# Layer 0's softmax in a four-layer graph kernel: one exponential over the whole tile, with the maximum subtracted and the rows summed by VectorE

## The chip, the cores and the metric

The kernel runs on one core of a Trainium2 chip. The metric is the device time of one execution in microseconds (us), as the median of several executions. A profile comes from one execution of its own, recorded by the hardware profiler. In it PE is TensorE (PEld its weight loads), DVE is VectorE, ACT is ScalarE, POOL is GpSimd and SP is SyncE; "L278" is line 278 of the kernel before the change.

## The reference, cut to what matters

Four graph layers stand one behind the other, each with a residual and a layer norm. `x` has 128 graphs of 64 nodes with 256 features, all float32. The change touches the first layer, a graph attention:

```python
def _L0_gnn_ref(h, adj_matrix, W, a):
    Wh = jnp.einsum('bnf,fo->bno', h, W)
    a1, a2 = (a[:Fout, 0], a[Fout:, 0])
    s1 = Wh @ a1
    s2 = Wh @ a2
    e = s1[:, :, None] + s2[:, None, :]
    e = jnp.where(e >= 0, e, ALPHA * e)
    e = jnp.where(adj_matrix[None] == 0, -jnp.inf, e)
    attention = jax.nn.softmax(e, axis=-1)
    return jnp.einsum('bij,bjo->bio', attention, Wh)
...
x = _layernorm(x + _L0_gnn_ref(x, adj, L0_gnn_W, L0_gnn_a), axis=-1)
x = _layernorm(x + _L1_gnn_ref(x, ...), axis=-1)
```

The second layer is an attention over a list of 512 edges with four heads; the third (two matrix products with batch normalisation) and the fourth (two graph products and LSTMs over windows) come later in time.

## The kernel before

The tokens are cut into 16 blocks of 512 (8 graphs). A block is four tiles of 128 tokens, each with two graphs, so that a softmax tile `e` of layer 0 is 128 partitions by 4 x 128 elements: in each of the four 128 x 128 pieces a row is one node and the columns are the nodes of two graphs, those outside the node's own graph and edges masked with -1e30.

Layer 0 of a block is cut into steps. `l0_a` (L238) brings the transposed input, `l0_b` (L247) makes `Wh` with the two scores, `l0_c` (L260) builds `e`: transposes on TensorE (L264), mask and sums on VectorE (L267), leaky ReLU (L269) and the negated row maximum `mx` (L271). `l0_x` (L274) is the exponential: ScalarE runs it four times, once for each 128 x 128 piece (L278), because its bias operand holds one number for each partition and each piece has its own maximum; each of the four also adds up its rows into `sm`. VectorE then takes the reciprocal `ri` (L281). `l0_d` (L283) transposes `e` on TensorE (L287) and copies it to SBUF (L289), and `l0_e` (L291) multiplies by `Wh` (L297), scales by `ri`, adds the residual (L300) and does the layer norm (`layernorm`, L88, with its last step on GpSimd, L100).

Layer 1 of a block: `l1_t` transposes the block (L227, L228); `l1_qv` makes, for half a block at a time, the queries (product L324, copies by ScalarE L334, subtractions by VectorE L335, small copies into `spad` L336) and the values (product L327, copy by ScalarE L337). `l1_graph` multiplies a graph's queries by the edge matrix (L361) into one of two PSUM buffers `z`, which ScalarE empties with a ReLU into `u` (L363); `reduce_heads` adds up the heads (L352). `l1_softmax`, `l1_sums` and `l1_weights` (L368 to L414) are the softmax over edges, once for two blocks. `v_m`, `v_a`, `v_b`, `v_c` (L416 to L474) apply the weights to the values of a block some rounds back: `v_a` is the product L432 and its copies `yT` (L436), `v_b` the product L446, the residual and a layer norm, `v_c` the product L467 for layer 2 and its copy (L471). All PSUM tiles but `z` and the edges' sums come from three banks named `m`, which are given out in turn, so that a product can wait for an earlier tile's last copy.

The order is written out by hand. The loop at L701 makes one round for each block q, with eight graph steps, and between two of them the steps listed in `between` (L703): in one round layer 1's graphs of block q, layer 1's queries and values of block q+1, and layer 0 of block q+2 stand side by side. `step` (L679) ties each step behind the last TensorE instruction of the step before it. Otherwise the instructions of an engine are put in order by a scheduler at build time, by readiness and the order of the code; at run time each engine works off its own list in order. Where `l0_x` stands depends on the round:

```python
def behind(do, q):
    if q < NQ:
        with tc.issue_after([t for t in nc.cur_bb.bb.instructions
                             if t.engine == mybir.EngineType.Activation][-1]):
            do(q)
```

S is q // 2 - 1 in even rounds and -1 in odd ones. In rounds with S >= 0 (even q from 2 on) `l0_x` is put behind the latest ScalarE instruction that was written, which is the values' copy of the first half block (L337). In the others (odd q, and q = 0) it is a step of its own ahead of the queries. The softmaxes of blocks 0 and 1 run ahead of the loop.

Of the kernel before, what the change touches and what calls it, by code (L numbers as in the profile page):

```python
# [8 lines left out]
F32 = mybir.dt.float32  # L9
F32R = mybir.dt.float32r  # L10
I32 = mybir.dt.int32
AF = mybir.ActivationFunctionType
OP = mybir.AluOpType
AX = mybir.AxisListType
# [3 lines left out]
P = 128  # L18
# [9 lines left out]
PQ = 4  # L28
# [13 lines left out]
def kernel(ctx: ExitStack, tc: tile.TileContext, i, out):  # L42
    nc = tc.nc

    const = ctx.enter_context(tc.tile_pool(name="const", bufs=1))
    small = ctx.enter_context(tc.tile_pool(name="small", bufs=4))
# [83 lines left out]
    with ExitStack() as two:  # L130
# [13 lines left out]
        def bank(shape, name="m", bufs=3):  # L144
            return (psm if name == "m" else ps).tile([P] + shape, F32, name=name, bufs=bufs)
# [71 lines left out]
        def own(q, shape, name):  # L217

            return work.tile(shape, F32, name=name, bufs=1) if q else su.tile(shape, F32, name)
# [16 lines left out]
        L0 = {}  # L236
# [37 lines left out]
        def l0_x(q):  # L274
            e, mx = L0[q]["e"], L0[q]["mx"]
            sm = small.tile([P, PQ], F32, name="sm")
            for c in range(PQ):
                nc.scalar.activation(e[:, c, :], e[:, c, :], AF.Exp, bias=mx[:, c:c + 1],  # L278
                                     accum_out=sm[:, c:c + 1])
            ri = L0[q]["ri"] = small.tile([P, PQ], F32, name="ri")  # L280
            nc.vector.reciprocal(ri, sm)  # L281

        def l0_d(q):  # L283
            e = L0[q]["e"]
            p_ = bank([PQ, P])
            for c in range(PQ):
                nc.tensor.transpose(p_[:, c, :], e[:, c, :], ident)  # L287
            eT = L0[q]["eT"] = own(q, [P, PQ, P], "eT")
            nc.scalar.activation(eT, p_, AF.Copy)  # L289
# [76 lines left out]
        ld, sm = {}, {}  # L366
# [202 lines left out]
        setup_order()  # L569
        l0_c(0)  # L570
        l0_x(0)
        l0_a(1)
        setup_ends()
        l0_b(1)
        l0_d(0)
        setup_gather()
        setup_queries()
        l0_e(0)
        l0_c(1)
        l0_x(1)  # L580
        setup_signs()
        l0_d(1)
        l1_t(0)
        l1_qv(0, 0)
# [94 lines left out]
        def step(do, n, *more):  # L679
            if not 0 <= n < NQ:  # L680
                return
            traced = nc.cur_bb.bb.instructions
            first = len(traced)
            if queue:
                with tc.issue_after(queue[-1]):
                    do(n, *more)
            else:
                do(n, *more)
            mine = [t for t in traced[first:] if t.engine == mybir.EngineType.PE]
            queue.extend(mine[-1:])  # L690
# [6 lines that stand above are left out]
# [4 lines left out]
        for q in range(NQ):  # L701
            S = q // BPS - 1 if q % BPS == 0 else -1
            between = [  # L703
                [(l0_e, q + 1), (l0_a, q + 2)],
                [(sums, q if q else -1), (l1_softmax, S)],
                [(l1_sums, S), (l0_b, q + 2)],
                [(v_b, q - LAG - 1)],
                [(l1_t, q + 1), (l1_weights, S), (l0_c, q + 2)] + [(l0_x, q + 2)] * (S < 0),
                [(sums, q), (l1_qv, q + 1, 0)] + [(lambda n: behind(l0_x, n), q + 2)] * (S >= 0),
                [(v_c, q - LAG - 1), (v_a, q - LAG)],  # L710
                [(l0_d, q + 2), (l1_qv, q + 1, 1)],
            ]
            for b in range(GQ):
                step(l1_graph, q, b)
                for do, n, *more in between[b]:
                    step(do, n, *more)
                if setup:
                    setup.pop(0)()
        sums(q)
        S = NQ // BPS - 1  # L720
# [256 lines left out]
        q = NQ - LAST - 1  # L977
# [16 lines left out]
        bias = wd.tile([P, SKIP, 8], F32, name="bias")  # L994
# [1010 lines left out]
```

## Time and profile before

| | before |
|---|---|
| median of 3 runs | 2036.22 us (2034.6 to 2041.47) |
| the profiled execution | 2039.12 us |
| its span from first to last instruction | 2037.3 us |
| granted TensorE clock, mean | 0.985 |
| TensorE busy | 1940.1 us (95%) |
| VectorE, ScalarE, GpSimd busy | 1248.0, 988.0, 880.0 us |
| four exponentials of all blocks, L278 | 64 of 390 ns (median), and 64 accumulator reads of 187 ns |
| row maximum, L271 | 16 of 685 ns |
| reciprocal, L281 | 16 of about 175 ns, VectorE idle 20.2 us before them |

The loop of layers 0 and 1 lies between about 66 and 560 us of the span, and a round takes about 30 us. A line of the timeline gives the start and the length in us, the engine, the line of the kernel, the operation, the tiles written and read, their shapes and how many; in square brackets stands how long the engine was idle before it and whose result ended that. A row of the groups ends with the busy time in all, the mean of one in ns, and the idle time before such instructions with the releasers.

### The profile page before, as it was taken

The page shows a single profiled execution, that of the slowest core. Times are in us where ns is not written, and L with a number is a line of the kernel's source. Part 1 is how long each engine was busy: PE and PEld are TensorE (multiplying, and loading weights), DVE is VectorE, ACT ScalarE, POOL GpSimd, SP SyncE. Part 2 cuts the span into 40 slices and gives each one's busy share as a digit, 9 for nine tenths or more (in the row PEclk, how much of TensorE's full clock was granted, in tenths as well). Part 3 has the DMA queues.
Part 4 walks back from the last instruction along what each step waited for, and adds up shares of the span by engine and source line. Part 5 has one row for each costly group of instructions (what it writes and reads, how often), then busy time and mean ns, then how long its engine had stood idle before and what let it go on. Part 6 is the DMA issues. An engine that isn't in the chain of part 4 may idle for free.

```text
span 2037.3 us, 31496 instructions
## 1 busy us (share of the span) xinstructions
PE 1940.1 (95%) x11447; PEld 1337.8 (66%) x11447; DVE 1248.0 (61%) x2763; ACT 988.0 (48%) x1892; POOL 880.0 (43%) x1017
## 2 busy tenths in 40 slices
PE   5999999999999999899999999999999999999996
PEld 4667777766554445477678577667577668578685
DVE  7456565565456555765557865557775557664566
ACT  2766666666345633644343644333544333543333
POOL 1123333333445544564645543435543445444264
PEclk8999999999999998999999999999999999999999
DMA  5344443332302025433243243133143032132022
GB/s 129 85 67 65 83 68 55 66 45 39 51 22 60 38 93 185 148 139 107 86 162 92 66 155 136 39 132 88 58 152 121 24 111 66 47 119 78 0 62 73
DMA packets 236539, 173.84 MB, mean 85 GB/s; under 512 B 150624, under 2 KB 213600, under 8 KB 233056
## 3 DMA queue, kind: packets, MB, share of 16 engines
q1 hardware_dynamic: 234528, 169.86, 29.5%
q8 instruction: 90, 1.47, 0.3%
q0 software_dynamic: 1024, 1.05, 0.2%
q10 hardware_dynamic: 832, 0.92, 0.1%
q14 instruction: 65, 0.53, 0.1%
HBM read 110.18 MB, written 61.60 MB: 84 GB/s over the span
## 4 chain that ended last, share of the span: by engine, by line
PE 73%; DVE 14%; ACT 5%; DMA 3%; issue 3%; POOL 2%; SPq 1%; DVEq 0%; POOLq 0%; ACTq 0%
PE l L1728 27%; PE l L1684 8%; PE pz L845 4%; PE l L1463 4%; PE m L253 3%; PE pz L774 3%; PE m L324 3%; PE e L352 2%; PE m L446 2%; PE g L1362 2%; PE m L327 2%; PE z L361 2%; PE g L1350 2%; PE pz L1043 2%; DVE cell L1642 1%
## 5 line engine op out<-in xcount | busy, mean ns | idle before, releaser
L1728 PE MATMUL l<-hs,wh 128*128 128x256 f32 (+1 forms) x896 | 276.0, 399 | 3.7 <-DVE hs L1592 3.1
L1728 PE MATMUL l<-xs,wx 128*128 128x256 f32 (+1 forms) x896 | 276.2, 399 | 2.9 <-DVE gate L1747 2.7
L1743 ACT ACTIVATE kept<-l 128x256 f32<-128x256 f32 (+1 forms) x224 | 88.8, 403 | 333.2 <-PE l L1728 331.8
L86 POOL TENSOR_TENSOR ln_rs<-ln_rs,mhalf 128x2 f32<-128x2 f32 (+2 forms) x98 | 85.5, 873 | 367.4 <-DVE ln_rs L98 366.9
L1728 PE MATMUL l<-H,wx 128*128 128x256 f32 (+1 forms) x672 | 210.5, 402 | 4.3 <-DVE gate L1756 3.4
L1728 PE MATMUL l<-hid,wh 128*128 128x256 f32 (+1 forms) x672 | 208.7, 399 | 0.0
L1728 PEld LDWEIGHTS l<-hs,wh 128*128 128x128 f32 x896 | 169.1, 190 | 47.1 <-DVE hs L1592 5.7
L1728 PEld LDWEIGHTS l<-xs,wx 128*128 128x128 f32 x896 | 168.9, 190 | 46.1 <-issue 2.8
L1761 ACT ACTIVATE gate<-gate,bias 128x512 f32<-128x512 f32 (+1 forms) x280 | 170.6, 657 | 40.7 <-DVE gate L1752 34.8
L1684 PE MATMUL l<-H,wx 128*128 128x256 f32 (+5 forms) x672 | 185.2, 431 | 4.9 <-DVE H L116 2.7
L363 ACT ACTIVATE u<-z 128x1024 f32<-128x1024 f32 x128 | 130.3, 1026 | 68.8 <-PE z L361 67.7
L1684 PEld LDWEIGHTS l<-H,wx 128*128 128x128 f32 x672 | 118.8, 190 | 65.5 <-issue 34.2
L1728 PEld LDWEIGHTS l<-H,wx 128*128 128x128 f32 x672 | 125.7, 190 | 42.6 <-DVE gate L1756 7.4
L1728 PEld LDWEIGHTS l<-hid,wh 128*128 128x128 f32 x672 | 127.2, 190 | 32.0 <-issue 2.9
L1751 POOL TENSOR_TENSOR gate<-gate,kept 128x256 f32<-128x256 f32 (+1 forms) x84 | 65.1, 775 | 144.9 <-DVE kept L1749 136.2
L335 DVE TENSOR_TENSOR qs<-m,qs 64x256 fp32r<-64x256 f32 x128 | 54.0, 422 | 106.3 <-ACT qs L334 104.4
L361 PE MATMUL z<-gath_r,qs 128*128 128x512 f32 x256 | 100.4, 480 | 9.3 <-ACT u L363 8.9
L1756 DVE TENSOR_TENSOR gate<-l,gate 128x256 f32<-128x256 f32 (+1 forms) x112 | 50.0, 446 | 88.4 <-POOL gate L1751 64.3
L1596 POOL TENSOR_TENSOR hs<-hid 128x256 f32<-128x256 f32 (+1 forms) x28 | 26.0, 929 | 170.1 <-DVE hid L1628 87.0
L1650 ACT ACTIVATE gate<-cell 128x512 f32<-128x512 f32 (+1 forms) x88 | 58.6, 666 | 83.6 <-DVE cell L1642 61.5
L1638 POOL TENSOR_TENSOR cell<-gate,cell 128x512 f32<-128x512 f32 (+1 forms) x56 | 75.4, 1367 | 28.4 <-ACT gate L1761 28.4
L1745 DVE TENSOR_TENSOR gate<-l,kept 128x256 f32<-128x256 f32 (+1 forms) x112 | 49.1, 438 | 59.7 <-ACT gate L1761 32.6
(380 smaller groups left out, 4097.6 us busy)
## 6 DMA issues: line engine op xcount, KB each, us to landing
wx<-sums SPq DMA_DIRECT2D x9, 2048.0 KB
wh<-sums SPq DMA_DIRECT2D x9, 1792.0 KB
way<-st SPq DMA_DIRECT2D x54, 256.0 KB
st<-way SPq DMA_DIRECT2D x216, 64.0 KB
xin<-in_x SPq DMA_DIRECT2D x16, 512.0 KB
ld<-table SPq DMA_DIRECT2D x16, 512.0 KB
x_dram<-y SPq DMA_DIRECT2D x16, 512.0 KB
x2r<-x_dram SPq DMA_DIRECT2D x32, 256.0 KB
```

Of the source, the lines that this page charges most:

```text
L86: nc.gpsimd.tensor_tensor(dst, dst, mhalf[:, :n], OP.pow)
L253: nc.tensor.matmul(p_, xT[:, k, c * P:(c + 1) * P], w0[:, k, :], start=k == 0, stop=k == KD - 1)
L361: nc.tensor.matmul(z[:, k, :], L1[q]["qs"][c][:, s, k * P:(k + 1) * P], gath_r, start=True, stop=True)
L363: nc.scalar.activation(u, z, AF.Relu)
L845: nc.tensor.matmul(self.bank[at], lhs, rhs, start=first and n == 0, stop=n == len(self.terms) - 1, skip_group_check=True)
L1463: nc.tensor.matmul(self.bank[at], lhs, rhs, start=new, stop=True, skip_group_check=True)
L1638: nc.gpsimd.tensor_tensor(c, t, c, OP.mult)
L1684: nc.tensor.matmul(b, w.raw[0][:, k, at, m, :], x, start=k == 0, stop=k == KD - 1)
L1728: nc.tensor.matmul(self.banks[j], lhs, rhs, start=src == 0, stop=src == 1)
L1743: nc.scalar.activation(self.keep(j), b, AF.Copy)
L1751: e.tensor_tensor(t[0][:, 1], t[0][:, 1], k[5], OP.add)
L1761: given(lambda: nc.scalar.activation(dst, dst, f, bias=b))
```

## The change

In the loop (q from 2 on) VectorE adds the negated maximum to the whole tile `e`, the maximum being repeated along each row of 128; ScalarE does one exponential over 128 x 512 without bias and without row sums; and VectorE sums the rows, in `l0_d`, ordered behind the VectorE instruction that was written last, and takes the reciprocal there. Blocks 0 and 1, ahead of the loop, keep the old form. In all rounds `l0_x` is now put behind the values' copy, so in odd rounds and round 0 too.

```diff
         def l0_x(q):
             e, mx = L0[q]["e"], L0[q]["mx"]
             sm = small.tile([P, PQ], F32, name="sm")
-            for c in range(PQ):
-                nc.scalar.activation(e[:, c, :], e[:, c, :], AF.Exp, bias=mx[:, c:c + 1],
-                                     accum_out=sm[:, c:c + 1])
+            if q < 2:
+                for c in range(PQ):
+                    nc.scalar.activation(e[:, c, :], e[:, c, :], AF.Exp, bias=mx[:, c:c + 1],
+                                         accum_out=sm[:, c:c + 1])
+            else:
+                nc.vector.tensor_add(e, e, mx[:, :, None].to_broadcast([P, PQ, P]))
+                nc.scalar.activation(e, e, AF.Exp)
+            L0[q]["sm"] = sm
+
+        def l0_d(q):
+            e, sm = L0[q]["e"], L0[q]["sm"]
             ri = L0[q]["ri"] = small.tile([P, PQ], F32, name="ri")
-            nc.vector.reciprocal(ri, sm)
-
-        def l0_d(q):
-            e = L0[q]["e"]
+            if q < 2:
+                nc.vector.reciprocal(ri, sm)
+            else:
+                with tc.issue_after([t for t in nc.cur_bb.bb.instructions if t.engine == mybir.EngineType.DVE][-1]):
+                    nc.vector.reduce_sum(sm, e, axis=AX.X)
+                nc.vector.reciprocal(ri, sm)
             p_ = bank([PQ, P])
...
-                [(l1_t, q + 1), (l1_weights, S), (l0_c, q + 2)] + [(l0_x, q + 2)] * (S < 0),
-                [(sums, q), (l1_qv, q + 1, 0)] + [(lambda n: behind(l0_x, n), q + 2)] * (S >= 0),
+                [(l1_t, q + 1), (l1_weights, S), (l0_c, q + 2)],
+                [(sums, q), (l1_qv, q + 1, 0)] + [(lambda n: behind(l0_x, n), q + 2)],
```

## The prediction

> **What bounds the kernel now.** I read the page's busy slices first, then the busy times by stretch, TensorE's timeline with its idle times, ScalarE's timeline in one block of each kind, and last the price rows. Round q (a pass of the loop at L701) carries the softmax of block q+2, so it is 14 rounds, 0 to 13, that change, all between 66 and 470 us.
>
> ```profile
> PE   5999999999999999899999999999999999999996
> ACT  2766666666345633644343644333544333543333
> ```
>
> ```profile
> 274.00:305.00 31.00, 30.08 (x278) 22.05 (x274) 21.80 (x50) 20.54 (x46) 12.03 (x15) 1.00 0.25 51
> 305.00:336.00 31.00, 29.00 (x272) 21.66 (x269) 16.18 (x48) 20.36 (x45) 11.83 (x15) 1.00 0.45 73
> ```
>
> The first numbers after the length are TensorE, its weight loads, VectorE, ScalarE, GpSimd. TensorE is the bound: it idles 0.9 us in an odd round (274 to 305) and 2.0 us in an even one (305 to 336). ScalarE is busy two thirds of the time. So freed ScalarE time is worth only what it takes from those idle times. TensorE's timeline shows where they are:
>
> ```profile
> 78.74 0.65 PE L287 MATMUL m<-ident,e 128*128 128x128 f32 x4 [0.34 <-ACT v L337]
> 220.12 1.15 PE L324 MATMUL m<-wq,tT 128*128 128x260 f32 x4 [0.56 <-ACT yT L436]
> 250.96 0.75 PE L361 MATMUL z<-gath_r,qs 128*128 128x512 f32 x2 [1.79 <-ACT u L363]
> 252.37 2.10 PE L324 MATMUL m<-wq,tT 128*128 128x260 f32 x4 [0.22 <-ACT yT L436]
> ```
>
> Even rounds 4 to 12 lose 2.0 us here (1.79+0.22 in round 6), odd rounds 5 to 13 lose 0.56 (L324 at 220.12 in round 5; L361 follows u at 218.39 almost without a wait), all waiting for ScalarE. An even round (6) and an odd one (5) on ScalarE:
>
> ```profile
> 247.51 0.38 ACT L334 ACTIVATE qs<-m 64x256 fp32r<-64x256 f32 x1
> 247.91 0.40 ACT L278 ACTIVATE e<-e,mx 128x128 f32<-128x128 f32 x1
> 249.89 1.02 ACT L363 ACTIVATE u<-z 128x1024 f32<-128x1024 f32 x1
> 250.81 1.02 ACT L471 ACTIVATE A<-z 128x1024 f32<-128x1024 f32 x1
> 251.71 1.09 ACT L436 ACTIVATE yT<-m 128x512 f32<-128x512 f32 x2
> ```
>
> ```profile
> 213.55 0.39 ACT L278 ACTIVATE e<-e,mx 128x128 f32<-128x128 f32 x1
> 216.91 0.38 ACT L334 ACTIVATE qs<-m 64x256 fp32r<-64x256 f32 x1
> 217.32 1.02 ACT L363 ACTIVATE u<-z 128x1024 f32<-128x1024 f32 x1
> ```
>
> In the even round the four exponentials stand directly ahead of the u that TensorE waits for. In the odd round they run 3.4 us earlier, while ScalarE would otherwise wait for queries. This difference decides the forecast.
>
> **What the Trainium skill says.** "ScalarE: Activation LUTs", section "What ACT_TABLE_LOAD costs": an ACTIVATE takes about 280 ns + 0.833 ns per element with a pointer bias, 186 ns + 0.833 without, overlaps by 93 ns, and a table load takes 1283 ns. The trace agrees: 392 ns at 128 with bias (387 by the page), 630 at 512 without (613), load 1283. "SBUF — State Buffer", section "Who interferes with whom": a VectorE instruction with two SBUF inputs contends with GpSimd reads, a tensor_reduce doesn't. The trace fits: the two-input add L380 takes 868 ns beside GpSimd's L100, the same size with one input in PSUM (L373) 691. The price rows (after the bar: busy us, mean ns of one, idle before it):
>
> ```profile
> L278 ACT ACTIVATE e<-e,mx 128x128 f32<-128x128 f32 x56 | 21.8, 392 | 0.6 <-DVE mx L271 0.4
> L381 ACT ACTIVATE e<-e 128x512 f32<-128x512 f32 x7 | 4.4, 630 | 12.2 <-DVE e L380 12.2
> L271 DVE TENSOR_REDUCE mx<-e 128x4 f32<-128x512 f32 x14 | 9.6, 686 | 0.5
> L269 DVE SCALAR_TENSOR_TENSOR e<-e 128x512 f32<-128x512 f32 x14 | 9.8, 697 | 0.5
> L380 DVE TENSOR_TENSOR e<-e,dn 128x512 f32<-128x512 f32 x7 | 6.1, 868 | 0.2
> ```
>
> **The change, part by part.** *Prices.* Removed per block: four exponentials, started 0.39 apart and ended by a 0.19 accumulator read, 1.65 us of ScalarE. Added: one of 0.63. ScalarE is relieved of 1.0 us a block, 14 us in all. VectorE gains an add and a row sum. The sum is a reduction like L271, 0.69. The add's broadcast operand is not in this trace; it cannot be cheaper than L269's 0.69 and I bound it above by 0.95 (the slowest two-input row of this size, L116 on wh, 953 ns); I take 0.69 in even rounds, where GpSimd isn't in L100 at that moment, and 0.87 in odd ones, where L100 runs from 212.16 to 214.33. VectorE: +1.4 to 1.6 us a block, 21 us in all.
>
> *Order.* From the order of instructions on each engine of both kernels: TensorE and GpSimd are unchanged; on SyncE a few input loads swap places, all two blocks ahead of their use, taken as nothing (if a load came late, its cover of some 20 us would have to go). VectorE runs maximum, add, the remaining query subtractions, sum, reciprocal. On ScalarE the exponential now stands after the values' copy (L337) and the last query copy (L334) in every round, and u follows.
>
> *Even rounds 4 to 12.* In round 6 the maximum ends at 246.85, a subtraction at 247.30, so the add at about 248.03, only 0.1 after the old start of the exponentials. One exponential lets u start 0.54 later (0.63 less 0.09 overlap), 248.6 instead of 249.89. TensorE's wait of 1.79 falls to about 0.5. Next late is the chain u, small copy L336 (now behind u), A, yT: A moves from 250.81 to 249.85, so L324 starts at 251.4 instead of 252.37. Gain 0.95 a round, not 1.3; five rounds, **-4.75**. Were the add 0.95, the gain would be 0.7.
>
> *Round 2* has waits of 0.84 and 0.37 of the transposes L287 for the exponentials; with the exponential from 132.6 to 133.25 they end near 133.9 instead of 134.8: **-0.8**.
>
> *Odd rounds 5 to 13.* With the exponentials gone from the front, the queries' chain still ends where TensorE lets it: the second half's product starts at 213.93, its copy follows 1.08 later as in even rounds (215.01), then subtraction, L336 and the last copy at 216.05, values' copy 216.45, exponential 217.06, L336, u at 217.84. It was 217.32: u is 0.5 later, and L361 waits that long. A follows without the L336 that stood between, so it and yT are 0.2 later, and TensorE's L324 with them: **+1.0** in five rounds. Round 3, retimed in the same way, +0.3.
>
> *Rounds 0 and 1* have neither A nor yT, and the transposes L287 come early: 78.74 and 103.73, released by the values' copy. Now they wait for the exponential behind it: in round 1 it would run from 103.7 to 104.3, +0.65. In round 0 the exponential brings the table load of 1.28 us (needed after the logarithm at L645), which ran early and now stands after the last query copy (78.67): 79.95, then the exponential to 80.6: +1.9. Together **+2.55**.
>
> *The new wait.* The sum waits on VectorE for the exponential; behind it are the reciprocal and the second half's subtractions, which come 4 us later (VectorE idled 4.84 before the one at 254.92). The reciprocal's reader, L300, comes 9 us later. Cost nothing; without that idle time, up to 0.9 a block. The old wait of the reciprocal (20.2 us of VectorE idle in all) hid nothing either.
>
> **Sum.** -4.75-0.8+1.0+0.3+2.55 = -1.7 us. The profiled execution took 2039.12 (span 2037.3), 2.9 above the median of 2036.22; 2037.4 there, 2034.5 for the median. The later stages only move with it.
>
> **The rivals.** *ScalarE's whole saving arrives.* If what TensorE waits for is ScalarE's sum of work in every round, 14 rounds give 1.0 each: 2036.2-14 = 2022. For it: every wait above names ScalarE, and waits of up to 15.6 us are there (5 x 2.0 + 5 x 0.56 + 2.8 in rounds 0 to 3). Against it: odd rounds' exponentials fill idle ScalarE time. Half of it would be 2029.
>
> *Slower: the odd rounds' add is held up by GpSimd.* The first subtraction of the queries now stands behind the add on VectorE. By the chain above it may end as late as 213.95 before anything moves, so the add, from 213.0, decides at 0.94 us. If it waits until L100's four instructions are over (214.33), u starts at 218.9, 1.6 late, and L324 1.25 late instead of 0.2: +6.25 for five rounds, in sum +3.5, 2039.7. For it: L380 and L100 slow each other (L100 takes 801 ns in one place, 558 in another). Against: they interleave, L380 lost only 0.18.
>
> *It doesn't do what it says*, the waits being tied to something else: 2036.2. Against it: the order shows the exponential moved in all 14 rounds.
>
> **How the numbers follow.** Forecast 0.62 (2034.5, itself 2031 to 2038 by the add's bounds, 1.3 us, by halving or doubling the losses of rounds 0 and 1, and by the spread of the runs, 2034.6 to 2041.5). ScalarE's whole saving or half of it 0.22; slower 0.12; nothing 0.04. 0.3% is 6 us, about what a measurement of this kernel tells from no change: 2030.1 and 2042.3. Faster by more: 0.20 of the second case and a little of the first, 0.22; slower by more: half of the slower case, 0.07; the rest 0.71. The range reaches into both: 2028.5 to 2040.5.
>
> **What would show it.** Right: TensorE's idle before L361 in even rounds near 0.5 and before L324 near 0.5; in odd rounds 0.6 before L361 and 0.25 before L324; L287 waiting about 2 us for e in round 0, 0.6 in round 1; the add at 0.7 to 0.9. Wrong: odd rounds without any wait (first rival), or the add over 0.94 with late subtractions (second).

## The result and the profile after

Over 20 executions of each the changed kernel took 2032.99 us (median; 2030.11 to 2038.06) and the kernel before 2040.53 us (2034.03 to 2044.41). The ratio on record is 0.9971, with a 95% interval from 0.9962 to 0.998: about 6 us faster (the medians themselves are 7.5 us apart), where 1.7 was forecast. The profiled execution took 2033.86 us (span 2032.1) at a clock of 0.986; before it was 2039.12 (2037.3) at 0.985. Lines of the kernel after stand 10 lower in the file from `l0_d` on: L287 is now L297, L361 is L371, L324 is L334, L363 is L373, L436 is L446, L467 is L477; the exponential is L283, the add L282, the row sum L293.

The page's busy slices of TensorE and ScalarE, after:

```profile
PE   5899999998999989899999999999999999999996
ACT  2666666666345633634343644333544333543333
```

They hardly differ from those of before. What changed is too small for a slice of 51 us; the page's sums of busy time show the work that was exchanged: ScalarE 988.0 to 973.8 us (-14.2; 14 were forecast), VectorE 1248.0 to 1268.4 (+20.4; 21 were forecast). Busy time by stretches of 31 us, after (TensorE, its weight loads, VectorE, ScalarE, GpSimd), about an odd and an even round:

```profile
270.00:301.00 31.00, 29.86 (x274) 22.22 (x274) 23.19 (x51) 19.62 (x39) 12.40 (x14) 1.00 0.25 50
301.00:332.00 31.00, 29.86 (x278) 22.07 (x271) 18.36 (x53) 19.52 (x39) 12.66 (x17) 1.00 0.44 73
```

TensorE now idles 1.1 us in both kinds of round, where it was 0.9 and 2.0. Its timeline after, at the places that the prediction showed (rounds 0, 1, 5 and 6):

```profile
77.81 0.66 PE L297 MATMUL m<-ident,e 128*128 128x128 f32 x4 [2.14 <-ACT e L283]
103.11 0.66 PE L297 MATMUL m<-ident,e 128*128 128x128 f32 x4 [0.85 <-ACT e L283]
216.96 0.75 PE L371 MATMUL z<-gath_r,qs 128*128 128x512 f32 x2 [0.54 <-ACT u L373]
218.36 1.14 PE L334 MATMUL m<-wq,tT 128*128 128x260 f32 x4 [0.22 <-ACT yT L446]
248.02 0.75 PE L371 MATMUL z<-gath_r,qs 128*128 128x512 f32 x2 [0.61 <-ACT u L373]
249.75 1.14 PE L334 MATMUL m<-wq,tT 128*128 128x260 f32 x4 [0.54 <-ACT yT L446]
```

The 1.79 us ahead of u's reader in round 6 is 0.61, and the 0.22 ahead of L334 has grown to 0.54: the second in the chain is now what is late. In round 5 the wait for u, hardly there before, is 0.54. In round 0 the transposes wait 2.14 us. ScalarE and VectorE in round 6 and in round 5, after:

```profile
245.56 0.69 DVE L282 TENSOR_TENSOR e<-e,mx 128x512 f32<-128x512 f32 x1
246.29 0.63 ACT L283 ACTIVATE e<-e 128x512 f32<-128x512 f32 x1 [0.17 <-DVE e L282]
246.94 1.02 ACT L373 ACTIVATE u<-z 128x1024 f32<-128x1024 f32 x1
248.19 1.02 ACT L481 ACTIVATE A<-z 128x1024 f32<-128x1024 f32 x1
249.11 1.08 ACT L446 ACTIVATE yT<-m 128x512 f32<-128x512 f32 x2
```

```profile
210.25 2.59 POOL L100 TENSOR_SCALAR y<-y,ln_rs 128x256 f32<-128x256 f32 x4
211.11 0.78 DVE L282 TENSOR_TENSOR e<-e,mx 128x512 f32<-128x512 f32 x1
215.04 0.62 ACT L283 ACTIVATE e<-e 128x512 f32<-128x512 f32 x1
215.88 1.02 ACT L373 ACTIVATE u<-z 128x1024 f32<-128x1024 f32 x1
```

In round 5 the add ran beside GpSimd's L100 and took 0.78 us, and its own reader did not wait for it: the exponential starts 3.2 us after its end. The new operations by source line, after (the three numbers are least, median and most ns):

```profile
L282 DVE TENSOR_TENSOR e<-e,mx x14: 691/693/778, 71.4 to 451.7; 128x512 f32<-128x512 f32 x14
L283 ACT ACTIVATE e<-e x14: 622/630/632, 77.1 to 455.6; 128x512 f32<-128x512 f32 x14
L293 DVE TENSOR_REDUCE sm<-e x14: 685/686/689, 77.8 to 456.3; 128x4 f32<-128x512 f32 x14
```

**Where the profile's 5 us of span came from.** I cut the span at the first transpose of layer 0 in round 0 (L264 in both) and at the product L467/L477 that waits 0.99 us for the last block's layer norm. The stretch between them went from 440.91 to 436.35 us, -4.56. Before it the two profiles differ by -2.74 us in code that is the same (that transpose starts between 67.3 and 71.0 us in all 14 profiles that I have, so this is the spread of runs), and behind it by +2.0. This last part has a place in the traces. Shortly behind that product TensorE's clock falls to half; in the profile after it stays there for 10.24 us, in the profile before for the first 3.41 of them (in these lines TensorE, weight loads, VectorE, ScalarE and GpSimd are followed by the mean granted clock), first after, then before:

```profile
507.16:517.40 10.24, 8.32 (x84) 3.74 (x85) 0.00 (x0) 2.59 (x4) 2.08 (x3) 0.50 0.11 40
515.08:525.32 10.24, 8.69 (x97) 5.63 (x98) 2.47 (x3) 2.11 (x3) 3.65 (x5) 0.83 0.04 16
```

From that product to the end, the six of my 14 profiles with 10.24 us at half clock in this place take 1527.3 to 1528.6 us, and the eight others 1524.9 to 1525.6. Among the six is a variant of the kernel before (before_shift), among the eight a second profile of the changed kernel (after_again), so that the change is not what decides it. The loop is therefore the measure of the change. A round is read as the time from one block's product `wh`,`eT` (L297, now L307) to the next block's:

```
us to round    1     2      3     4     5     6      7     8     9     10     11    12    13
before       24.99 30.56* 24.31 32.25 28.55 33.70* 28.55 32.23 28.55 33.63* 28.54 32.24 28.54
after        25.31 29.23* 25.42 31.39 28.68 31.39  28.98 31.39 28.69 31.38  28.68 31.40 28.68
```

The first transpose to round 0's product went from 12.85 to 14.46. A star marks a round with a *spell* in which the granted clock is half for 3.41 us. This is the part that I had not reckoned with: rounds 6 and 10 of the kernel before have one (33.70 and 33.63 against 32.25 and 32.23, so 1.4 to 1.45 us each), and after they have none. The same stretches of round 6 show it, first before (TensorE, weight loads, VectorE, ScalarE, GpSimd; then the granted clock):

```profile
248.85:252.26 3.41, 1.50 (x30) 0.98 (x19) 0.18 (x1) 3.37 (x9) 0.96 (x1) 1.00 0.28 49
252.26:255.67 3.41, 3.30 (x8) 2.65 (x9) 0.42 (x1) 2.62 (x7) 0.96 (x1) 0.50 0.03 10
```

and after:

```profile
244.35:247.76 3.41, 3.06 (x133) 2.51 (x131) 3.01 (x7) 2.88 (x7) 0.00 (x0) 1.00 0.68 114
247.76:251.17 3.41, 2.60 (x13) 2.05 (x14) 0.09 (x1) 3.36 (x7) 0.96 (x1) 1.00 0.15 29
```

Before, a stretch in which TensorE worked 1.50 of 3.41 us is followed by one at a clock of 0.50. After, the stretches around the same wait have 3.06 and 2.60 us of work, and the clock stays at 1.00.

So two accounts were tested. *The account of the waits*: the prediction's steps, at their sizes, -1.7 us. *The waits with their spells*: the same, and on top the spells that a long wait of TensorE sets off, two of which are gone from this profile. The rivals were that ScalarE's saving arrives as such, that the move behind the values' copy is itself part of the gain, and that the gap is only the spread of runs.

### The profile page after: what moved, and what is told of

Its sections match the earlier page's. It is cut to its first block, busy times and chain, and to the rows that moved or that the text cites. A ratio compares the mean times of both kernels' runs of the same rounds, so it can differ in the third digit from the quotient of the medians.

```text
span 2032.1 us, 31437 instructions
## 1 busy us (share of the span) xinstructions
PE 1936.1 (95%) x11447; PEld 1334.1 (66%) x11447; DVE 1268.4 (62%) x2791; ACT 973.8 (48%) x1794; POOL 879.9 (43%) x1017
## 3 DMA queue, kind: packets, MB, share of 16 engines
q8 instruction: 90, 1.47, 0.3%
## 4 chain that ended last, share of the span: by engine, by line
PE 71%; DVE 16%; ACT 5%; issue 3%; DMA 3%; POOL 2%; SPq 1%; DVEq 0%; ACTq 0%; POOLq 0%
PE l L1738 27%; PE l L1694 8%; PE pz L855 4%; PE l L1473 4%; PE pz L784 3%; PE m L253 2%; PE e L362 2%; PE m L456 2%; PE m L334 2%; PE g L1372 2%; PE z L371 2%; PE g L1360 2%; PE pz L1053 2%; PE m L337 2%; DVE cell L1652 1%
## 5 line engine op out<-in xcount | busy, mean ns | idle before, releaser
L373 ACT ACTIVATE u<-z 128x1024 f32<-128x1024 f32 x128 | 130.4, 1025 | 69.5 <-PE z L371 68.5
L371 PE MATMUL z<-gath_r,qs 128*128 128x512 f32 x256 | 100.5, 480 | 5.9 <-ACT u L373 5.9
L1755 DVE TENSOR_TENSOR gate<-l,kept 128x256 f32<-128x256 f32 (+1 forms) x112 | 49.0, 438 | 59.6 <-ACT gate L1771 32.7
```

The lines of the kernel that those rows point to most:

```text
L371: nc.tensor.matmul(z[:, k, :], L1[q]["qs"][c][:, s, k * P:(k + 1) * P], gath_r, start=True, stop=True)
L373: nc.scalar.activation(u, z, AF.Relu)
```

## The experiments

Each ratio is to the kernel before on the same chip, with its 95% interval; diffs are against the changed kernel unless said otherwise. Runs of one chip: the first four experiments; the next four; before_again and best; before_shift and gap_8.

### One exponential, in the old place (one_exp)

```diff
-                [(l1_t, q + 1), (l1_weights, S), (l0_c, q + 2)],
-                [(sums, q), (l1_qv, q + 1, 0)] + [(lambda n: behind(l0_x, n), q + 2)],
+                [(l1_t, q + 1), (l1_weights, S), (l0_c, q + 2)] + [(l0_x, q + 2)] * (S < 0),
+                [(sums, q), (l1_qv, q + 1, 0)] + [(lambda n: behind(l0_x, n), q + 2)] * (S >= 0),
```

> The VectorE add, the single exponential and the VectorE row sum of the change, but the softmax step keeps its old place (ahead of the queries in odd rounds and in round 0). Theory A (the traces' sum: even rounds gain 0.86 us each at L324, while the move behind the values' copy costs about 2 us in rounds 0 and 1 and 0.15 in each odd round): even rounds as in the changed kernel (waits of 0.6 before L361 and 0.55 before L324), the transposes of rounds 0 and 1 wait under 0.4 us, odd rounds lose nothing; 2 to 3.5 us less than the changed kernel, so a ratio to before near 0.996 to 0.9955. Rival B (the move behind the values' copy is what pays): odd rounds as before, ratio 0.9985 or worse than the changed kernel's.

Measured: 2030.24 against 2035.85, ratio 0.9973 [0.9964, 0.9983]. In its profile odd rounds from 5 on take 28.17 us (before 28.55; round 7 alone takes 28.50), even ones from 4 on 31.39 as in the changed kernel. TensorE's timeline in round 5, where the only wait left is that for yT:

```profile
215.40 1.14 PE L334 MATMUL m<-wq,tT 128*128 128x260 f32 x4 [0.33 <-ACT yT L446]
```

The new softmax without the move gives the gain. In odd rounds the new place takes 0.5 us a round back (28.68 against 28.17).

### The new form only in even blocks from 4 on (even_only)

```diff
-            if q < 2:
+            if q < 4 or q % 2:
                 for c in range(PQ):
...
-            if q < 2:
+            if q < 4 or q % 2:
                 nc.vector.reciprocal(ri, sm)
```

and the steps in the old place, as in one_exp.

> The new form only in even rounds from 2 on; odd rounds and round 0 keep the four exponentials in their old place. Theory A: the whole gain is made in the even rounds, 5 x 0.86 + 0.2 to 0.8 in round 2, about 5 us, with none of the losses of rounds 0 and 1: 2.5 to 3 us less than the changed kernel. Rival B: odd rounds carry part of the gain, so that this is slower than the changed kernel by 2 us or more.

Measured: 2029.81, ratio 0.9975 [0.9963, 0.9986]. Even rounds from 4 on take 31.39 us, odd ones from 5 on 28.54 as before. With six exponentials changed of 14, ScalarE's saving is less than half of the whole, and yet the gain is that of one_exp within the interval. ScalarE's saved time is worth something where ScalarE is late, in the even rounds, and little elsewhere: the first rival of the prediction falls.

### Only the move: four exponentials, behind the values' copy in all rounds (move_only)

Against the kernel before:

```diff
-                [(l1_t, q + 1), (l1_weights, S), (l0_c, q + 2)] + [(l0_x, q + 2)] * (S < 0),
-                [(sums, q), (l1_qv, q + 1, 0)] + [(lambda n: behind(l0_x, n), q + 2)] * (S >= 0),
+                [(l1_t, q + 1), (l1_weights, S), (l0_c, q + 2)],
+                [(sums, q), (l1_qv, q + 1, 0)] + [(lambda n: behind(l0_x, n), q + 2)],
```

> The kernel before with its four exponentials and nothing else changed but the place: behind the values' copy in all rounds. Theory A: even rounds as before (1.8 before L361); in odd rounds from 5 on u comes 1.5 us later and L324 1.2 us later, in rounds 0 and 1 the transposes wait 2.9 and 1.6 us: 10 to 13 us slower than before, ratio near 1.005 to 1.0065. Rival B: the move alone gains, ratio under 1.

Measured: 2051.74, ratio 1.0069 [1.0056, 1.0083]: slower by 14 us, a little more than the 10 to 13 expected. TensorE's timeline in an odd and an even round:

```profile
230.56 0.73 PE L361 MATMUL z<-gath_r,qs 128*128 128x512 f32 x2 [1.67 <-ACT u L363]
262.81 0.73 PE L361 MATMUL z<-gath_r,qs 128*128 128x512 f32 x2 [1.78 <-ACT u L363]
```

The move gives odd rounds the very wait that even rounds had, and each takes 29.82 us instead of 28.55 (+1.27). Single spells appear in places where the kernel before had none. The move is a cost; with one exponential in place of four it shrinks to 0.51 us an odd round (28.68 in the changed kernel against 28.17 in one_exp). The two parts of the change don't add up: -0.38 for the new softmax alone and +1.27 for the move alone, but +0.13 together.

### The exponential in 16 pieces in even rounds (gap_16)

```diff
-                nc.scalar.activation(e, e, AF.Exp)
+                if q >= 4 and q % 2 == 0:
+                    for n in range(16):
+                        piece = e[:, n // 4, n % 4 * 32:(n % 4 + 1) * 32]
+                        nc.scalar.activation(piece, piece, AF.Exp)
+                else:
+                    nc.scalar.activation(e, e, AF.Exp)
```

> The changed kernel, but in even rounds (from 2 on) the exponential is cut into 16 pieces of 128x32, which gives ScalarE about 1.5 us more ahead of u: TensorE's wait before L361 is as long as before the change or longer (1.8 to 2.5 us). Theory C (waits of TensorE of about 1.8 us or more are at times followed by a spell of half clock of 3.4 us, which costs 1.2 to 1.7 us; before had two such spells behind even rounds' waits, the changed kernel none): the spells are back behind even rounds' waits, 1 to 4 of them, and the time is that of before or 1 to 5 us above it. Rival D (the spells fall where they fall): no spell behind these waits, and the time is 5 to 9 us above the changed kernel by the waits alone.

It was to bring the long wait back by another route. Measured: 2041.93, ratio 1.0025 [1.0018, 1.0031], against less than 1 for the changed kernel. The waits before u's reader came back at 1.1 to 2.3 us and even rounds rose to about 32.75 (33.65 in round 4), but only round 4 of the five has a spell. In rounds 4, 8, 10 and 12 some 0.4 us of TensorE's idle time stands earlier, in the products of `v_a` or `v_c`, with no releaser in the profile, and the wait before u's reader is shorter there. It says that the wait matters; it doesn't separate wait from spell.

### The changed kernel once more, and one_exp beside it (after_again, one_exp_b)

No edit: the changed kernel, and the text of one_exp.

> The changed kernel once more, on the same chip as the next two kernels. Theory A (waits, and spells of half clock apart from them): its rounds between the products L297 take 31.4 us (even) and 28.7 us (odd) as in its first profile, 1.5 to 3.5 us slower than one_exp, ratio to before 0.9985 to 0.997 according to how many spells before has on this chip. Rival (what the first comparison showed beyond 2 us lies in the waits): as fast as one_exp or faster, ratio 0.997 or less.

> one_exp once more (the single exponential in the old places), beside the changed kernel on the same chip. Theory A: 31.4 us (even) and 28.2 us (odd) between the products L297, about 7 us less than before over the 14 rounds without spells, ratio near 0.9965; faster than the changed kernel by 3 to 6 us. Rival: no faster than the changed kernel.

Measured: 2033.13 and 2029.03 against 2036.7, ratios 0.9981 [0.9973, 0.9988] and 0.997 [0.9959, 0.9981]. On this chip the change is worth 3.9 us, against 5.9 by the first ratio; the two intervals meet at 0.9973 to 0.998. one_exp is the faster of the two by about 4 us. The rounds of after_again repeat those of the changed kernel to about 0.1 us, with the exceptions of round 2 (27.95 for 29.23, without its spell) and of the stretch to round 0's product (16.06 for 14.46, with a spell at 69.7). No even round from 4 on has a spell in either; round 2 of one_exp_b has one (at 121.5).

### The exponential behind yT (late_exp)

In odd rounds and round 0 `l0_x` has its old place, as in one_exp. In the other even rounds it is put behind `v_a`'s list and the transposes behind the second half's queries and values:

```diff
-                [(l1_t, q + 1), (l1_weights, S), (l0_c, q + 2)],
-                [(sums, q), (l1_qv, q + 1, 0)] + [(lambda n: behind(l0_x, n), q + 2)],
-                [(v_c, q - LAG - 1), (v_a, q - LAG)],
-                [(l0_d, q + 2), (l1_qv, q + 1, 1)],
+                [(l1_t, q + 1), (l1_weights, S), (l0_c, q + 2)] + [(l0_x, q + 2)] * (S < 0),
+                [(sums, q), (l1_qv, q + 1, 0)],
+                [(v_c, q - LAG - 1), (v_a, q - LAG)] + [(lambda n: behind(l0_x, n), q + 2)] * (S >= 0),
+                [(l1_qv, q + 1, 1), (l0_d, q + 2)] if S >= 0 else [(l0_d, q + 2), (l1_qv, q + 1, 1)],
```

> As one_exp, and in even rounds from 2 on the exponential goes behind ScalarE's copies of yT and the transposes of e go behind the second half's queries and values, so that neither u, A and yT nor the banks stand behind the exponential. Theory A (in even rounds what is left, 0.6 before L361 and 0.55 before L324, is the sum of ScalarE's work up to yT): these two waits go, a wait of up to 0.5 us for eT comes before the product with Wh; even rounds 30.5 to 30.9 us instead of 31.4, 3 to 5 us faster than one_exp, ratio near 0.9945. Rival: the transposes moved behind make eT late by 1 us or more and the even rounds stay at 31.4 or above.

Measured: 2035.69, ratio 1.0 [0.9991, 1.0008]. The waits before L371 and L334 are indeed gone from even rounds, and nothing is won. TensorE's timeline in round 6 shows the new wait:

```profile
252.82 0.66 PE L297 MATMUL m<-ident,e 128*128 128x128 f32 x4 [1.53 <-ACT v L347]
```

The transposes wait for the values' copy, which they don't read: `m`'s three banks go round, and by the order of the products the values' bank is the one that they get. Even rounds from 4 on take 32.1 to 32.7 us. This is a miss of the account of the waits as I used it to design the run: I moved a step past two waits and did not ask which bank it would then be given.

### The table load ahead of the loop (table_early)

```diff
             nc.scalar.activation(lb, pl, AF.Ln, bias=eps8)
+            nc.scalar.activation(sel[:, 0:1], sel[:, 0:1], AF.Exp)
```

> The changed kernel with a one-element exponential right behind the logarithm of setup, so that the table load of round 0 runs there instead of behind the last query copy. Theory A (1.28 of round 0's wait of 2.14 us before the transposes is the table load): the wait falls to about 0.85 as in round 1; up to 1.2 of it may come back before L264 or L324, since the transposed block is copied behind the load. Rival (the wait has another cause): it stays above 1.8.

A single execution, 2031.43 us. Round 0's transposes, on TensorE's timeline:

```profile
78.95 0.66 PE L297 MATMUL m<-ident,e 128*128 128x128 f32 x4 [0.85 <-ACT e L283]
```

The wait fell from 2.14 to 0.85 us, by about the 1.28 of the load, and the stretch to round 0's product from 14.46 to 13.18. A function of one element drew the load to an idle place, so most of the loss of round 0 (1.3 of 1.6 us) was the load's place and not the exponential's.

### The kernel before once more (before_again), and the best of the parts (best)

The first is unedited; the second is one_exp with the line of table_early.

> The kernel before once more, unchanged, as the measure of what two runs of the same kernel differ by, and for a second look at where its spells of half clock lie. Ratio 1.000, within 0.001. Theory C (a wait of TensorE of 1 us or more can set off a spell): any spell between 130 and 470 us begins within 3 us behind one of the even rounds' waits of 1.5 to 1.8 us; 0 to 3 of them. Rival D: spells also begin elsewhere in the rounds.

> one_exp with the one-element exponential behind the setup's logarithm of table_early: the single exponential in its old places and the table load out of round 0's queries. Theory A: round 0's wait of 1.0 us (L324, for the values' copy behind the table load) goes; 0.5 to 1 us less than one_exp, about 7.5 us less than before without spells, ratio 0.9965 to 0.9955. Rival: the load only moves to the copies of the transposed block, and the time is that of one_exp, 0.997.

Measured: 2040.86 and 2025.86 against 2038.19, ratios 1.0008 [0.9996, 1.002] and 0.9941 [0.9923, 0.9959]. An unedited kernel differs from itself by at most 0.2%. The four spells of before_again begin within 0.2 us of those of the first profile (122.7, 252.4, 375.3, 484.5 against 122.6, 252.3, 375.1, 484.4), so in these two they fall alike; the timed executions differ more (last part of the next section). best beats both kernels: its loop takes 426.79 us (before 440.91), with even rounds from 4 on of 31.39, odd ones from 5 on of 28.16 and not a spell in that stretch. It gained some 12 us where 7.5 without spells were expected.

### The kernel before, pushed against the grid (before_shift)

All spells of a profile begin at whole multiples of 3.413 us from each other (in the kernel before 38.0, 36.0 and 32.0 steps). If a fixed grid decides which of the equal waits gets a spell, a shift of all later rounds must change which ones do. Against the kernel before:

```diff
                 nc.scalar.activation(e[:, c, :], e[:, c, :], AF.Exp, bias=mx[:, c:c + 1],
                                      accum_out=sm[:, c:c + 1])
+            if q == 3:
+                for _ in range(3):
+                    nc.scalar.activation(e, e, AF.Copy)
```

> The kernel before, with three redundant in-place copies of e (0.6 us each) behind the exponentials of round 1 only, so that all later rounds run about 1 to 1.6 us later and are otherwise the same. Theory C (the spells of half clock start on a fixed grid of 3.41 us, and which of the even rounds' equal waits is followed by one depends on where it falls on the grid): the spells leave rounds 6 and 10; other rounds get them, or none; their number decides the time, 1.45 us each. Rival D (a spell belongs to the work of a certain round): rounds 6 and 10 keep their spells, at positions 1 to 1.6 us later.

Measured: 2041.88, ratio 1.0 [0.9989, 1.0012]. Round 6 kept its spell, round 10 lost it, and round 12, which had none before, got one (the round takes 33.76 us). The number stayed two of five. Here are the stretches of the grid that hold the waits of rounds 6, 10 and 12:

```profile
251.51:254.92 3.41, 1.44 (x26) 0.93 (x16) 0.18 (x1) 3.37 (x9) 0.96 (x1) 1.00 0.28 49
374.39:377.80 3.41, 1.85 (x41) 1.34 (x41) 0.18 (x1) 3.36 (x9) 0.48 (x2) 1.00 0.06 14
435.83:439.24 3.41, 1.61 (x8) 1.21 (x9) 0.18 (x1) 3.39 (x8) 0.96 (x1) 1.00 0.03 10
```

Read against the grid, the push missed its aim: the rounds came 2.6 us later and the grid itself 0.8 us earlier, together one whole step. In rounds 4 to 10 the wait before u's reader therefore ends as far into its stretch as before, to 0.1 us (in round 6, 2.05 us for 2.11), and that round 6 kept its spell says nothing against the grid. Round 10 stands where it stood, but its wait is 1.54 us here for 1.75, with 1.85 us of TensorE work in the stretch for 1.65. Since it has no spell, round 12 comes 1.4 us earlier on the grid (its wait ends 1.6 us into the stretch for 3.0), and with a wait of the same 1.75 us it gets one. That one round is what this run shows of the grid; neither expectation came out whole.

### The exponential in 8 pieces in even rounds (gap_8)

As gap_16, with eight pieces of 64.

> The changed kernel with the exponential of even rounds cut into 8 pieces of 128x64, some 0.6 to 0.9 us more ahead of u than the single one. Theory A: the wait before L361 is near 1.3 us instead of 0.6, that before L324 0.3 to 0.5; an even round takes 31.8 to 32.3 us instead of 31.4; 3 to 5 us above the changed kernel, near before or up to 2 us above it. Theory C: spells behind even rounds' waits only if they fall rightly on the grid, 0 to 2.

Measured: 2038.93 against 2041.26, ratio 0.9996 [0.9986, 1.0007]. The pieces bring waits of 1.28 to 1.55 us back before u's reader, and with them two spells in five even rounds, in rounds 6 and 10. Here are the stretches that precede them and those of rounds 8 and 12, which have none:

```profile
247.74:251.15 3.41, 1.63 (x8) 1.22 (x9) 0.86 (x2) 3.39 (x8) 0.96 (x1) 1.00 0.19 37
309.19:312.60 3.41, 1.87 (x61) 1.45 (x53) 0.94 (x3) 3.36 (x11) 0.96 (x1) 1.00 0.08 22
370.62:374.03 3.41, 1.63 (x15) 1.15 (x9) 0.87 (x2) 3.39 (x8) 0.43 (x1) 1.00 0.00 1
432.05:435.47 3.42, 1.88 (x69) 1.56 (x59) 1.05 (x3) 3.37 (x12) 0.86 (x1) 1.00 0.04 10
```

The waits of these four rounds are alike (1.54 to 1.55 us); in rounds 6 and 10 they end 1.6 us into their stretch of the grid, in rounds 8 and 12 they end 2.3 to 2.4 us into it, where more of the work falls into the same stretch. With the rest of the change in place, the wait alone brings the spells back: rounds 6 and 10 take 33.53 and 33.57 us, the even rounds without a spell 32.02. Most of the gain is gone with waits and spells together. This run ties the spells to the shortened wait, and their choice among equal waits to the grid. (The interval still touches that of after_again at 0.9986 to 0.9988, so the loss of the gain is shown by the rounds more than by the medians.)

## Why the prediction was right, and where its sizes were off

The forecast of 2034.5 us lies 1.5 above the measured median, inside its range of 2028.5 to 2040.5. That nearness flatters it and is in part luck: the kernel before was also slower in this measurement than in the runs shown (2040.53 against 2036.22), and the difference forecast, 1.7 us, was 3.9 to 5.9. Step by step, with the loop's rounds as the measure:

| step | forecast, us | in the profile, us |
|---|---|---|
| even rounds 4 to 12 | -4.75 | -4.2 (spells taken out) |
| round 2 | -0.8 | -1.3 |
| odd rounds 5 to 13 | +1.0 | +1.0 |
| round 3 | +0.3 | +1.1 |
| round 0 | +1.9 | +1.6 |
| round 1 | +0.65 | +0.3 |
| from there to the loop's end | 0 | -0.15 |
| sum of the waits | -1.7 | -1.7 |
| spells of rounds 6 and 10 | not in the sum | -2.9 (2 x 1.45) |
| the loop | -1.7 | -4.56 |

That the waits sum to the forecast -1.7 is luck too, for terms missed by -0.5 to +0.8 cancel. What held, but for round 3, is which waits go, which come, and the engine behind each.

- **Even rounds.** The waits named came out as forecast: 0.61 before L371 and 0.54 before L334, against 0.5 and 0.5. The round gains 0.86 instead of 0.95, the difference being these tenths. One of them is the overlap of 0.09 us that the sum took off the exponential: in round 6, u starts 0.65 us after the exponential's start (246.94 and 246.29), not 0.54. The step "Gain 0.95 a round, not 1.3" held: the second member of the chain, yT, is what is late next.
- **Odd rounds.** 0.54 and 0.22 against 0.6 and 0.25; four of the five lose 0.14 where 0.2 was forecast, and round 7 lost 0.43 (28.98), so that the +1.0 is met by chance. The extra 0.3 can be followed in the trace:

```profile
267.44 2.05 POOL L429 COPY am<-ld 128x1024 f32<-128x1024 f32 x1 [4.98 <-DMA ld<-table]
268.97 0.55 DVE L85 TENSOR_SCALAR ln_rs<-ln_mv 128x4 f32<-128x4 f32 x1
```

  GpSimd's copy waited for a transfer and so lay beside a small VectorE step of the layer norm, which took 0.55 us for the 0.16 of other rounds and ended with the copy. The add, 0.4 us late behind it, held up the first query subtraction, and u came 0.3 later. Of the 70 odd rounds from 5 on in my 14 profiles the same is seen in round 7 of after_again, one_exp and one_exp_b (0.65, 0.52 and 1.00 us for this step) and in no other. It is the path of the prediction's second rival, by another delay than the add's own.
- **The add, the sum, the exponential.** 693 ns (778 beside GpSimd), 686, 630: at the low end of the bounds of the add. The Trainium skill's page "SBUF — State Buffer", section "Who interferes with whom", says that VectorE with two SBUF inputs contends with GpSimd's reads; the trace agrees, with 0.09 us, half of what I took for odd rounds. The second rival needed an add of 0.94 us and falls by that number.
- **The new wait on VectorE.** It idles 7.0 us in all ahead of the 14 sums, and of the other engines only GpSimd waits for a sum, once, for 2.0 us: it cost nothing, as said.
- **Rounds 0, 1 and 2.** The waits of rounds 0 and 1 are 2.14 and 0.85; the table load is the larger part of the first, as table_early shows. Round 2 has a spell in both profiles, so that its -1.3 is not the waits' alone.
- **Round 3** is a term that I mis-sized, +1.1 for +0.3. I retimed the chain of u and did not see that the small copy L346, now behind the exponential and u, is the last reader of a bank of `m`. On TensorE's timeline after, the transposes wait for it:

```profile
157.68 0.66 PE L297 MATMUL m<-ident,e 128*128 128x128 f32 x4 [0.65 <-ACT spad L346]
```

  This wait is 0.65 of the 0.8 us missed; the rest I did not trace. It is the same kind of oversight as in late_exp.
- **The term that was missing.** "Five rounds, -4.75" priced a wait at its own length. Rounds 6 and 10 of the kernel before also paid 1.45 us each for the half clock that followed, and in the profile after this went with the wait. The slices of the page rounded it off, and I did not look at the clock in finer stretches: the four spells were in the trace, and 33.7 against 32.2 us for rounds of the same work would have led there. How much of this each execution saves is another matter (below).
- **"The later stages only move with it."** In this profile they took 2.0 us more, by the longer stretch at half clock shown above, which falls in some profiles of both kernels.
- **First rival**, ScalarE's whole saving: refuted by odd rounds that got longer, and by even_only. **It does nothing**: refuted by both ratios.

**How much the spells are worth outside the profile.** The record has the mean granted clock of the timed executions of every set but one: only those of the kernel before in the first comparison lack it. Within one kernel the time goes with this clock: 0.001 of it is 4.1 us at half clock (worked out from a span of 2037 us), or 1.2 spells, and goes with about 1.5 us in the kernel before. So executions of the two kernels can be compared at the same clock. Here are the means of 128 executions of the kernel before (those measured beside the experiments, and before_again) and 37 of the changed one (the first comparison and after_again):

| mean granted clock | before, us (executions) | changed, us (executions) |
|---|---|---|
| 0.988 | 2034.4 (25) | 2031.9 (17) |
| 0.987 | 2036.3 (36) | 2033.4 (9) |
| 0.986 | 2037.0 (16) | 2034.8 (4) |
| 0.985 | 2038.3 (17) | 2034.4 (3) |
| 0.983 | 2042.1 (21) | 2038.1 (1) |

At the same clock the change is worth 2 to 3 us where there are most executions (on the chip of after_again alone 2.1 at 0.988 and 3.1 at 0.987). The rest of its gain goes with the clock. On that chip the means are 0.9875 and 0.9867, so that the changed kernel saved about one spell an execution and not the two of the profiles. The kernel before has a mean of 0.987 on two of the chips and of 0.985 on the two others, so its spells are not the same in every execution. one_exp, in its first measurement, gained its 5.6 us at a clock no higher than that of the kernel before (0.9865 against 0.9871): there the clock has no part in the gain. best, on a chip where the kernel before stood low, gained 6.4 and 8.7 us at the same clock (0.985 and 0.988), near the 7.5 expected of its waits, though from few executions; the rest of its 12 goes with the clock.

What stays open: 2 to 3 us at the same clock is about a microsecond more than the waits' 1.7, and no run shows where it lies. An equal mean clock also doesn't say that the spells stand in the same places.

## What to carry to other kernels

Price a wait of the bound engine from the chain of the engine it waits for, and take what is late next as the limit of the gain; this gave the waits of rounds 5 to 13 to about 0.1 us, but missed one of 0.65 us in round 3. Then look at the granted clock in stretches as short as the wait, since a long wait may cost a second time behind its end, and compare executions at the same mean clock. When a step is moved on an engine, ask not only who waits for its result but which buffer its neighbours now free later, and what it carries with it, a table load for instance.

## What the runs showed of the hardware

**Half clock follows a stretch of little work.** I laid a grid of 3.413 us, fixed by each profile's own spells, over the stretch from 62 to 500 us of all 14 profiles that I had, and read TensorE's busy time in each of the 1,762 stretches that are not themselves at half clock. All 20 with less than 1.55 us of TensorE work are followed by a spell; of those between 1.55 and 2.22 us, 17 of 65; of the 1,677 above, none. Behind 500 us, where the two borders were not drawn from, it is 42 of 47, 11 of 48 and none of 6,054; the five of the 47 all stand about 16 us before the end of their profiles. Two of the kernel before that are not followed by one, rounds 8 and 12:

```profile
310.32:313.73 3.41, 1.65 (x78) 1.42 (x71) 0.44 (x2) 3.36 (x11) 1.16 (x2) 1.00 0.05 14
433.17:436.58 3.41, 1.65 (x86) 1.47 (x77) 0.54 (x2) 3.36 (x11) 0.29 (x1) 1.00 0.06 14
```

and round 10's, which is:

```profile
371.74:375.14 3.40, 1.65 (x41) 1.16 (x32) 0.18 (x1) 3.35 (x9) 0.96 (x1) 1.00 0.10 27
```

The same 1.65 us of matmuls: round 10 has fewer of them, fewer weight loads (1.16 against 1.42 and 1.47 us) and less work of VectorE. None of this is the rule, though. A stretch of best with still fewer matmuls and as few loads is not followed by a spell, and in gap_8 above two with 0.86 and 0.87 us of VectorE are:

```profile
116.80:120.21 3.41, 1.65 (x13) 1.17 (x11) 2.56 (x2) 3.38 (x7) 0.55 (x2) 1.00 0.36 113
```

So what decides between 1.55 and 2.22 us stays open. In the changed kernel no stretch about the waits of the even rounds 4 to 12 has less than 2.25 us, as in the first of these lines:

```profile
367.23:370.64 3.41, 2.25 (x52) 1.72 (x45) 0.86 (x2) 3.34 (x7) 0.96 (x1) 1.00 0.08 24
473.03:476.44 3.41, 1.33 (x10) 0.78 (x7) 3.28 (x4) 2.28 (x4) 0.60 (x2) 1.00 0.00 0
```

The second is the stretch at the loop's end, where a wait of 2.24 us for VectorE remains and is followed by a spell in this profile. The Trainium skill's page "TensorE: Matmul & The Clock Gate", section "Part 1: The HAM clock gate (the "warmup" mystery)", describes a monitor of TensorE's activity that sets the clock to half or full in a window of 3413 ns that runs freely. The grid and the 0.50 agree. The same page's rule, in "HAM oscillation — how this bites in real kernels", of no idle gaps over about 3.4 us, is not enough here: waits of 1.5 to 1.8 us were followed by spells where they and some short idle times fell into one window. This reading was made after the runs, from their traces; gap_16 and gap_8 were made to test the link between wait and spell and before_shift the grid, and no run set out to test the limit.

**A bank given out in turn costs as much as a wait for data.** Moving one small reader of `m` behind other work made a wait of 0.65 us in round 3, and moving the transposes one of 1.27 to 1.53 us in the even rounds of late_exp, in both cases with nothing in the data that asked for it.
